# Layer 2 of a four-layer stack: where the second half's expert rows are gathered, and in which order the outputs are summed

## The chip, the cores and the metric

The kernel runs on one core of one Trainium2 chip. The metric is the device time of one launch in microseconds (us); the time before is the median of three runs. A core has five engines that each execute their own stream of instructions in order: PE (matmul, with its weight load shown as PEld), DVE (vector), ACT (scalar and activation), POOL (GpSimd) and SP, which here only issues transfers. They are tied together by semaphores. A transfer is issued by an engine (SP for plain ones, POOL for indirect ones, which take the row numbers from a tile) and carried out by the DMA queues.

## The reference, cut to what matters

x has 2048 tokens (four sequences of 512) of 256 features, all in float32. Each of four layers computes `x = x + attn(xn) + ffn(xn)` from the layernorm xn of x. The change is in layer 2:

```python
# attn: each token mixes its own 16 heads, with one key and one value
attn = softmax(einsum('blhd,bld->blh', q, k) / sqrt(hd))
out = (attn[..., None] * v[:, :, None, :]).reshape(b, l, -1)

# ffn: 8 experts, the best two for each token, and a shared one
scores = softmax(einsum('th,eh->te', xf, gate_w), axis=-1)
topk_w, topk_i = top_k(scores, 2)
topk_w = topk_w / sum(topk_w)
eo = einsum('eti,eih->eth', silu(xf @ wg) * (xf @ wu), wd)
y = einsum('te,eth->th', cw, eo)       # cw: topk_w at topk_i, else 0
shared = silu(xf @ sg) * (xf @ su) @ sd
x = x + out + y + shared
```

Layer 3 then does a causal attention with 16 heads of 128 and eight experts of another kind on the new xn.

## The kernel before, in words

x lies in SBUF as 16 tiles of 128 tokens by 256 features; a sequence is four tiles. `xnT` is the transposed layernorm, in SBUF too, from which most matmuls are fed. The normalised rows xn are also written to DRAM, as `xn_half`, one for each half of the tokens (1024).

**The experts of layer 2 by halves.** The `Half` object of each half routes its tokens (`dispatch`, L1248). It sorts the 2048 choices of 1024 tokens by expert into 23 slots of 128 rows (NS = 23): `ids` says which token each row of a slot takes, `expert` which weights a slot uses, `slot` where each token's two results lie, and `weight` what they are multiplied by. `experts` (L1366) works through the slots in twelve pairs (the last one is a single slot):

- `gather(j)` (L1373): POOL issues two indirect transfers (L1376), each of 128 rows of `xn_half` into the tile `xs`, of which there are three buffers. The gathers of pairs 0 and 1 are issued ahead of the loop, that of pair j + 2 at the start of step j.
- `turn(j)` (L1381): four PE transposes (L1386) and an ACT copy to `xsT` (L1391).
- `hidden(j)` (L1393): eight matmuls (L1398), the activation `gate` on ACT (L1405), the product `hs` on DVE (L1406).
- `turn_hidden(j)` (L1408): two PE transposes (L1412), an ACT copy to `hsT` (L1414).
- `down(j)` (L1416): four matmuls (L1420), a DVE copy to `os` (L1425), and SP's store to DRAM, `slots_out` (L1427).

`combine` (L1456) brings the results back: for each of the half's eight tiles and each of two choices POOL gathers 128 rows of `slots_out` into `row` (L1463, four buffers), and `add_scaled` (L147) adds row times weight to x on DVE (L153). When a sequence has all its sums, `part_done` starts its layernorm for layer 3 (L94: statistics on DVE at L102 and L103, the root on ACT at L90, xn on DVE at L110; later PE transposes at L121 and ACT copies to xnT).

`head_mix` (L1149) is the attention of layer 2 for one sequence: four times four matmuls (L142) with the bias added into `qkv` on DVE (L1161), a product (L1166) and a sum on DVE, a softmax, then the product `prod` on POOL (L1178), which DVE adds to x (L1183).

**The order of the work.** `weave` (L215) interleaves generators: each yields the cost of what it has just emitted, the one that has used the smallest share of its total goes next, and a start value above 0 makes a stream begin later. Layer 2 (`run`, L1500) weaves the shared expert with the two dispatches; then the first half's experts with the head mix; then the second half's experts with the first half's combine. Layer 3 (L1551) weaves the second half's combine (`rest`, L1526) with its attention and its experts. From the program so written a scheduler decides the order of each engine's instructions by its own estimates; `keep_in_program_order` ties an instruction to its place as written. On the chip every engine then follows its order strictly: an instruction that waits holds up all behind it.

At the start of layer 3 `full_attention` (L1037) computes V by projections (L142), the keys and queries of a head (L134; the bias of the queries is added on DVE, L1057), the scores (L628) and, on DVE and ACT, the softmax (L631, L635).

Of the kernel before, what the change touches and what calls it, by code (L numbers as in the profile page):

```python
# [12 lines left out]
ALU = mybir.AluOpType  # L13
AX = mybir.AxisListType

P = 128
NB, SEQ, DM = 4, 512, 256
# [65 lines left out]
def v3(ap, b):  # L83
    return ap.rearrange("p (a b) -> p a b", b=b)
# [62 lines left out]
def add_scaled(c, t, part, w=None):  # L147

    x = c.x[:, t, :]
    if w is None:  # L150
        c.nc.vector.tensor_add(x, part, x)  # L151
    else:
        c.nc.vector.scalar_tensor_tensor(x, part, w, x, ALU.mult, ALU.add)  # L153


def silu_times(c, pool, out, gate, other):
# [58 lines left out]
def weave(c, *streams, flush=True):  # L215

    live = [[start * total, total, gen] for gen, total, start in streams]
    while live:  # L220
        s = min(live, key=lambda s: s[0] / s[1])
        cost = next(s[2], None)
        if cost is None:
            live.remove(s)
        else:
            s[0] += cost
        c.step()
    if flush:
        c.step(True)
# [998 lines left out]


E8, HT, NS = 8, NTILE // 2, 23  # L1230
EW = 6 * P


class Half:
# [3 lines left out]

    def __init__(self, c, k, pool, keep, dram, hf, xn):
        self.c, self.k, self.pool, self.hf, self.xn = c, k, pool, hf, xn  # L1240
        self.out = c.tile(dram, [NS * P, DM], "slots_out")
        new = lambda shape, tag, dtype=F32: c.tile(keep, shape, tag, dtype, bufs=2)
        self.ids = new([P, NS], "ids", U32)
        self.slot = new([P, 2 * HT], "slot", U32)
        self.weight = new([P, 2, HT], "weight")
        self.expert = new([P, NS], "expert", I32)

    def dispatch(self):  # L1248
# [75 lines left out]
        for i in range(2 * HT + 4):  # L1324
# [25 lines left out]
        nc.vector.tensor_scalar(  # L1350
            where[:1], where[:1], float(E8 - 1), float(EW), ALU.min, ALU.mult
        )
# [10 lines left out]
        nc.vector.tensor_mul(w, w, tot[:, None, :].to_broadcast([P, 2, HT]))  # L1363
        yield 1.0

    def experts(self, weights, xpool, pool, opool):  # L1366


        c, nc = self.c, self.c.nc
        pairs = [[t for t in (2 * j, 2 * j + 1) if t < NS] for j in range((NS + 1) // 2)]  # L1370
        xs, xsT, hs, hT = {}, {}, {}, {}

        def gather(j):  # L1373
            xs[j] = c.tile(xpool, [P, 2, DM], "xs", bufs=3)
            for i, t in enumerate(pairs[j]):
                nc.gpsimd.indirect_dma_start(  # L1376
                    out=xs[j][:, i, :], out_offset=None, in_=self.xn,
                    in_offset=bass.IndirectOffsetOnAxis(ap=self.ids[:, t : t + 1], axis=0),
                )

        def turn(j):  # L1381
            pt = c.ps("tr")
            n = len(pairs[j])
            for i in range(n):
                for d in range(2):
                    nc.tensor.transpose(  # L1386
                        pt[:, (2 * i + d) * P : (2 * i + d + 1) * P],
                        xs[j][:, i, d * P : (d + 1) * P], c.ident,
                    )
            xsT[j] = c.tile(pool, [P, 4, P], "xsT", bufs=2)  # L1390
            nc.scalar.copy(xsT[j][:, : 2 * n, :], v3(pt[:, : 2 * n * P], P))  # L1391

        def hidden(j):  # L1393
            ph = v3(c.ps(), 2 * P)
            n = len(pairs[j])
            for i, t in enumerate(pairs[j]):
                for d in range(2):
                    nc.tensor.matmul(  # L1398
                        ph[:, i, :], lhsT=xsT[j][:, 2 * i + d, :],
                        rhs=weights[:, bass.ds(where[t] + 2 * d * P, 2 * P)],  # L1400
                        start=(d == 0), stop=(d == 1),
                    )
            sg = c.tile(pool, [P, 2, P], "gate", bufs=2)
            hs[j] = c.tile(pool, [P, 2, P], "hs", bufs=2)
            nc.scalar.activation(sg[:, :n, :], ph[:, :n, :P], AF.Silu)  # L1405
            nc.vector.tensor_mul(hs[j][:, :n, :], sg[:, :n, :], ph[:, :n, P:])  # L1406

        def turn_hidden(j):  # L1408
            pt = c.ps("tr")
            n = len(pairs[j])  # L1410
            for i in range(n):
                nc.tensor.transpose(pt[:, i * P : (i + 1) * P], hs[j][:, i, :], c.ident)  # L1412
            hT[j] = c.tile(pool, [P, 2, P], "hsT", bufs=2)
            nc.scalar.copy(hT[j][:, :n, :], v3(pt[:, : n * P], P))  # L1414

        def down(j):  # L1416
            po = v3(c.ps("acc"), DM)
            n = len(pairs[j])
            for i, t in enumerate(pairs[j]):
                nc.tensor.matmul(  # L1420
                    po[:, i, :], lhsT=hT[j][:, i, :],
                    rhs=weights[:, bass.ds(where[t] + 4 * P, DM)], start=True, stop=True,
                )
            os = c.tile(opool, [P, 2, DM], "os", bufs=2)
            nc.vector.tensor_copy(os[:, :n, :], po[:, :n, :])  # L1425
            rows = self.out[2 * j * P : (2 * j + n) * P, :]
            nc.sync.dma_start(rows.rearrange("(i p) d -> p i d", p=P), os[:, :n, :])  # L1427

        where = []
        N = len(pairs)  # L1430
        gather(0)
        gather(1)
        for lo in (0, 12):
            where.extend(nc.values_load_multi_w_load_instructions(
                self.expert[:1, lo : min(lo + 12, NS)], engines=[mybir.EngineType.PE],
                min_val=0, max_val=(E8 - 1) * EW,
                skip_runtime_bounds_check_because="the chip has limited them to the last expert's",
            )[1])
        turn(0)
        yield 0.5  # L1440
        for j in range(N + 2):
            if j + 2 < N:
                gather(j + 2)
            if j < N:
                hidden(j)
                yield 1.7
            if j + 1 < N:
                turn(j + 1)
            if j >= 2:
                down(j - 2)  # L1450
                yield 0.9
            if 1 <= j <= N:
                turn_hidden(j - 1)
            yield 0.6

    def combine(self, pool):  # L1456

        c, nc = self.c, self.c.nc
        for t in range(HT):
            tt = self.hf * HT + t  # L1460
            for r in range(2):
                row = c.tile(pool, [P, DM], "row", bufs=4)
                nc.gpsimd.indirect_dma_start(  # L1463
                    out=row, out_offset=None, in_=self.out,
                    in_offset=bass.IndirectOffsetOnAxis(
                        ap=self.slot[:, r * HT + t : r * HT + t + 1], axis=0
                    ),
                )
                add_scaled(c, tt, row, self.weight[:, r, t : t + 1])
            if tt % TPB == TPB - 1:  # L1470
                c.part_done(tt // TPB)
            yield 1.0


class Layer2:
# [23 lines left out]

    def run(self):  # L1500
        c, a = self.c, self.a
        xs, self.rows = self.pool("t_xs"), self.pool("t_rows")
        with ExitStack() as stack:
            temp, mixer = self.pool("t_temp", stack), self.pool("h_t", stack)
            unit = c.unit(a["t_shared"])
            h_small = c.tile(mixer, [P, 864], "h_small")
            c.nc.sync.dma_start(h_small, a["h_unit"])

            def dispatch():
                for half in self.halves:  # L1510
                    yield from half.dispatch()

            def mix():
                for b in range(NB):
                    yield from head_mix(c, mixer, h_small, b)

            shared = glu_pieces(c, mixer, [unit], n=2, width=256, loaded=True, bufs=4)
            experts = [half.experts(self.weights, xs, temp, self.rows) for half in self.halves]
            weave(c, (shared, 41.0, 0.0), (dispatch(), 34.0, 0.0), flush=False)
            weave(c, (experts[0], 40.0, 0.0), (mix(), 12.0, 0.0), flush=False)  # L1520
            weave(
                c, (experts[1], 40.0, 0.0), (self.halves[0].combine(self.rows), 10.0, 0.0),
                flush=False,
            )

    def rest(self):  # L1526
        yield from self.halves[1].combine(self.rows)
        self.stack.close()
# [22 lines left out]
def layer3(c, a, ahead, store):  # L1551


    def attention():
        yield from full_attention(c, a)

    def rest():
        yield from ahead
        c.parts(2, store)

    weave(
        c, (rest(), 110.0, 0.0), (attention(), 765.0, 0.0), (top_p_experts(c, a), 765.0, 0.95)
    )


# [192 lines left out]
```

## Time and profile before

| | |
|---|---|
| median of three runs | 3229.73 us |
| the three runs | 3223.44, 3234.39, 3229.73 us |
| the profiled execution | 3223.57 us, of which the span 3221.7 us |
| mean granted clock of PE | 0.988 |
| first half's experts and head mix | about 1624.5 to 1683.6 us from the span's start |
| second half's experts and first half's combine | about 1683.6 to 1749.3 us |
| indirect gathers of expert rows, L1376 | 46 on POOL, 946 ns each at the median, 3.5 us from issue to landing |
| indirect gathers of result rows, L1463 | 32 on POOL, 2.7 us from issue to landing |

The span is one execution on the chip, seen by the hardware profiler. Layer 2's experts are a small part of it, some 125 us; layers 0 and 1 lie before, layer 3 behind them. A timeline row gives the start, the duration, the engine, the line and operation, what is written from what, and in brackets how long the engine had been idle before it and what ended that. In the waits view a row names who waited, for what, how many us in total, how often, and the longest.

### The profile page before, as it was taken

Reading aid. Unit: us, or ns where it says so; the run is one execution under the profiler, and the core shown is the slowest. Engines: PE = TensorE matmul, PEld = TensorE weight load, DVE = VectorE, ACT = ScalarE, POOL = GpSimd, SP = SyncE. Lnnn points to the kernel's source line nnn. Section 1 sums busy time; section 2 is a strip of 40 time slices with the busy share of each in tenths; the row PEclk is TensorE's granted clock in tenths of the full one; section 3 lists DMA queues with packets and bytes.
Section 4 is the critical chain, followed back from the end, with each engine's and each line's share of the span. In section 5 each row is a group of like instructions: output and inputs, shape, how many; then the busy total and the mean of one; then the engine's idle time right before and its main releaser. Section 6 shows DMA issues by size and latency. Waiting matters only on the chain.

```text
span 3221.7 us, 35846 instructions
## 1 busy us (share of the span) xinstructions
PE 3099.8 (96%) x12502; PEld 1887.7 (59%) x12502; DVE 1857.9 (58%) x4730; ACT 1262.2 (39%) x2911; POOL 655.5 (20%) x525
## 2 busy tenths in 40 slices
PE   8999999998899999999997999999999999999999
PEld 4565656565555555555575565665665665555555
DVE  4777878887676777777654655545545522222222
ACT  4444444443456566657433433333333411111111
POOL 0465556556200132322044000000000000000000
PEclk9999999999999999999998999999999999999999
DMA  3232323322201244434133000000000000000000
GB/s 128 76 112 95 124 86 105 111 86 93 91 23 31 54 136 95 111 78 138 54 102 118 8 1 27 1 27 1 16 5 1 20 20 20 20 20 20 0 0 27
DMA packets 88947, 183.59 MB, mean 57 GB/s; under 512 B 14176, under 2 KB 57200, under 8 KB 84160
## 3 DMA queue, kind: packets, MB, share of 16 engines
q1 hardware_dynamic: 74304, 133.48, 12.8%
q0 software_dynamic: 14176, 47.01, 5.9%
q8 instruction: 99, 1.62, 0.2%
q10 hardware_dynamic: 288, 0.82, 0.1%
q14 instruction: 80, 0.66, 0.1%
HBM read 159.38 MB, written 12.98 MB: 53 GB/s over the span
## 4 chain that ended last, share of the span: by engine, by line
PE 73%; DVE 12%; DMA 6%; POOL 4%; ACT 3%; issue 2%; SPq 1%; DVEq 0%; ACTq 0%; POOLq 0%
PE mm L134 28%; PE acc L204 9%; PE mm L628 8%; PE mm L142 5%; PE acc L1092 4%; PE acc L644 3%; DMA G<-own 3%; DVE cy L269 2%; DVE G L410 2%; PE tr L1084 2%; PE tr L807 2%; PE acc L851 2%; PE acc L864 2%; DMA psw<-pes 1%; POOL y L459 1%
## 5 line engine op out<-in xcount | busy, mean ns | idle before, releaser
L134 PE MATMUL mm<-xnT,wu 128*128 128x512 f32 x2128 | 956.4, 596 | 7.9 <-DVE cy L269 3.4
L134 PEld LDWEIGHTS mm<-xnT,wu 128*128 128x128 f32 x2128 | 400.1, 191 | 462.7 <-issue 433.8
L635 ACT ACTIVATE pr<-pr,nm 128x128 f32<-128x128 f32 (+3 forms) x512 | 286.0, 559 | 313.3 <-DVE nm L631 310.9
L196 ACT ACTIVATE sg<-mm 128x512 f32<-128x512 f32 x168 | 99.9, 595 | 600.3 <-PE mm L134 600.1
L197 DVE TENSOR_TENSOR hT<-sg,mm 128x512 f32<-128x512 f32 x168 | 115.0, 684 | 376.1 <-PE mm L134 364.9
L204 PE MATMUL acc<-wu,hT 128*128 128x256 f32 x1344 | 304.8, 380 | 0.6 <-DVE hT L197 0.5
L631 DVE CUSTOM_DVE_ANT_0 pr<-mm,late 128x128 f32<-128x128 f32 (+3 forms) x512 | 244.6, 482 | 88.9 <-PE mm L628 84.3
L204 PEld LDWEIGHTS acc<-wu,hT 128*128 128x128 f32 x1344 | 252.2, 190 | 53.6 <-issue 20.4
L134 PE MATMUL mm<-xnT,w_in 128*128 128x512 f32 x512 | 231.5, 596 | 6.7 <-DVE cy L269 5.1
L968 POOL DMA_INDIRECT e<-in_p_experts,ids x128 | 128.1, 1001 | 494.9 <-DVE x L153 463.6
L410 DVE TENSOR_TENSOR_SCAN G<-G,eye 128x1024 f32<-128x1024 f32 x64 | 157.9, 2468 | 53.5 <-DMA G<-own 53.5
L628 PE MATMUL mm<-k,q 128*128 128x128 f32 (+3 forms) x512 | 181.0, 444 | 5.1 <-DVE q L1057 5.1
L628 PE MATMUL mm<-kf,qf 128*128 128x128 f32 (+3 forms) x512 | 176.9, 445 | 8.9 <-DVE qf L786 6.4
L436 POOL TENSOR_TENSOR G<-G,CB 128x1024 f32<-128x1024 f32 x64 | 151.1, 2361 | 141.0 <-ACT CB L362 77.6
L269 DVE SCALAR_TENSOR_TENSOR cy<-mm,ws,cy 128x509 f32<-128x509 f32 (+2 forms) x216 | 158.3, 741 | 26.2 <-ACT cy L265 22.7
L422 ACT ACTIVATE xD<-xc,ws 128x128 f32<-128x128 f32 x256 | 84.3, 391 | 198.6 <-POOL y L459 192.7
L134 PEld LDWEIGHTS mm<-xnT,w_in 128*128 128x128 f32 x512 | 96.4, 191 | 111.2 <-issue 96.5
L153 DVE SCALAR_TENSOR_TENSOR x<-acc,cw,x 128x256 f32<-128x256 f32 x128 | 61.9, 484 | 155.6 <-PE acc L204 155.6
L151 DVE TENSOR_TENSOR x<-acc,x 128x256 f32<-128x256 f32 x176 | 73.9, 421 | 134.2 <-PE acc L644 103.5
L1092 PE MATMUL acc<-PT,V 128*128 128x512 f32 (+3 forms) x512 | 149.5, 433 | 0.0
L1057 DVE TENSOR_SCALAR q<-mm,bias 128x512 f32<-128x512 f32 x64 | 48.0, 750 | 163.0 <-PE mm L134 163.0
L807 PEld LDWEIGHTS tr<-con,pr 128*128 128x128 f32 x640 | 80.9, 143 | 90.3 <-ACT pr L800 32.1
(306 smaller groups left out, 5032.3 us busy)
## 6 DMA issues: line engine op xcount, KB each, us to landing
G<-own SPq DMA_DIRECT2D x64, 512.0 KB, 4.2
w_in<-in_m_units SPq DMA_DIRECT2D x16, 1024.0 KB, 5.0
eb<-since SPq DMA_DIRECT2D x96, 128.0 KB, 3.3
wu<-in_o_units SPq DMA_DIRECT2D x8, 1536.0 KB, 6.7
wo<-in_m_units SPq DMA_DIRECT2D x16, 512.0 KB, 3.9
psw<-pes SPq DMA_DIRECT2D x128, 64.0 KB, 2.6
wu<-in_f_units SPq DMA_DIRECT2D x4, 1536.0 KB, 6.6
wu<-in_l_units SPq DMA_DIRECT2D x4, 1408.0 KB, 8.4
```

The costliest lines, as they stand in the source:

```text
L134: c.nc.tensor.matmul(out, lhsT=w[:, d, cols], rhs=c.xnT[:, d, tokens], start=(d == 0), stop=(d == 1))
L142: c.nc.tensor.matmul(out, lhsT=c.xnT[:, d, tokens], rhs=w[:, d, cols], start=(d == 0), stop=(d == 1))
L204: nc.tensor.matmul(po, lhsT=hT[k][:, t * P : (t + 1) * P], rhs=wd[:, k, :], start=(i == 0), stop=(i == per - 1),)
L269: nc.vector.scalar_tensor_tensor(y[:, j:], src[:, : SEQ - j], conv[:, k, 3 - j : 4 - j], y[:, j:], ALU.mult, ALU.add,)
L410: nc.vector.tensor_tensor_scan(flat, flat, eye.rearrange("p h t -> p (h t)"), 0.0, ALU.mult, ALU.add)
L436: nc.gpsimd.tensor_mul(G, G, seqs[b][2][:, t, :][:, None, :].to_broadcast([P, HG, P]))
L628: nc.tensor.matmul(sc, lhsT=q[:, i * P : n], rhs=k[:, :n], start=True, stop=True)
L631: nc.vector.tensor_tensor_reduce(out=pr, in0=sc, in1=late[:, SEQ - n :], scale=1.0, scalar=-NEG, op0=ALU.add, op1=ALU.min, accum_out=nm,)
L635: nc.scalar.activation(pr, pr, AF.Exp, bias=nm, scale=-1.0, accum_out=total)
L807: nc.tensor.transpose(pt[:, (i - j) * P : (i - j + 1) * P], prs[s][i][:, j * P : (j + 1) * P], c.ident)
L968: nc.gpsimd.indirect_dma_start(out=e, out_offset=None, in_=a["p_experts"], in_offset=bass.IndirectOffsetOnAxis(ap=ids[:, t, k : k + 1], ax ...
L1092: nc.tensor.matmul(z[:, j * P :], lhsT=head["V"][:, j, h, :], rhs=head["PT"][:, j, j * P :], start=(j == 0), stop=(j == TPB - 1),)
```

## The change

The first half's rows are still gathered inside its own experts, two pairs ahead, with three buffers (tag `xs0`). The second half's rows have twelve buffers of their own (tag `xs1`, one for each pair), and the generator that gathers them is a third stream beside the first half's experts and the head mix, with a total of 12 and start 0. Nothing is gathered inside the second half's experts any more. The pool of these buffers is now closed together with those of the experts and the mixer, at the end of `run`. In `combine` there are six row buffers instead of four, and the adds to x are tied to the order as written. The weights of the streams change a little: the first half's combine has a total of 11 instead of 10 and starts at 0.2 of it; the second half's combine, in layer 3, starts at 0.012 of its total.

```diff
-        c.nc.vector.tensor_add(x, part, x)
-    else:
-        c.nc.vector.scalar_tensor_tensor(x, part, w, x, ALU.mult, ALU.add)
+        return c.nc.vector.tensor_add(x, part, x)
+    return c.nc.vector.scalar_tensor_tensor(x, part, w, x, ALU.mult, ALU.add)
...
 E8, HT, NS = 8, NTILE // 2, 23
+PAIRS = [[t for t in (2 * j, 2 * j + 1) if t < NS] for j in range((NS + 1) // 2)]
...
+        self.xs = {}
...
-    def experts(self, weights, xpool, pool, opool):
-        def gather(j):
-            xs[j] = c.tile(xpool, [P, 2, DM], "xs", bufs=3)
-            for i, t in enumerate(pairs[j]):
-                nc.gpsimd.indirect_dma_start(
-                    out=xs[j][:, i, :], out_offset=None, in_=self.xn,
+    def gather(self, pool, bufs, js):
+        for j in js:
+            x = self.xs[j] = self.c.tile(pool, [P, 2, DM], f"xs{self.hf}", bufs=bufs)
+            for i, t in enumerate(PAIRS[j]):
+                self.c.nc.gpsimd.indirect_dma_start(
+                    out=x[:, i, :], out_offset=None, in_=self.xn,
                     in_offset=bass.IndirectOffsetOnAxis(ap=self.ids[:, t : t + 1], axis=0),
                 )
+            yield 1.0
+
+    def experts(self, weights, pool, opool, more):
...
-        gather(0)
-        gather(1)
+        if more:
+            next(more)
+            next(more)
...
-            if j + 2 < N:
-                gather(j + 2)
+            if more:
+                next(more, None)
...
-                row = c.tile(pool, [P, DM], "row", bufs=4)
+                row = c.tile(pool, [P, DM], "row", bufs=6)
...
-                add_scaled(c, tt, row, self.weight[:, r, t : t + 1])
+                c.tc.keep_in_program_order(
+                    add_scaled(c, tt, row, self.weight[:, r, t : t + 1])
+                )
...
-        xs, self.rows = self.pool("t_xs"), self.pool("t_rows")
+        self.rows = self.pool("t_rows")
         with ExitStack() as stack:
-            temp, mixer = self.pool("t_temp", stack), self.pool("h_t", stack)
+            xs, temp, mixer = (self.pool(name, stack) for name in ("t_xs", "t_temp", "h_t"))
...
-            experts = [half.experts(self.weights, xs, temp, self.rows) for half in self.halves]
+            first, last = self.halves
+            every = range(len(PAIRS))
+            experts = [
+                half.experts(self.weights, temp, self.rows, more)
+                for half, more in ((first, first.gather(xs, 3, every)), (last, None))
+            ]
             weave(c, (shared, 41.0, 0.0), (dispatch(), 34.0, 0.0), flush=False)
-            weave(c, (experts[0], 40.0, 0.0), (mix(), 12.0, 0.0), flush=False)
             weave(
-                c, (experts[1], 40.0, 0.0), (self.halves[0].combine(self.rows), 10.0, 0.0),
-                flush=False,
+                c, (experts[0], 40.0, 0.0), (mix(), 12.0, 0.0),
+                (last.gather(xs, len(PAIRS), every), 12.0, 0.0), flush=False,
             )
+            weave(c, (experts[1], 40.0, 0.0), (first.combine(self.rows), 11.0, 0.2), flush=False)
...
-        c, (rest(), 110.0, 0.0), (attention(), 765.0, 0.0), (top_p_experts(c, a), 765.0, 0.95)
+        c, (rest(), 110.0, 0.012), (attention(), 765.0, 0.0), (top_p_experts(c, a), 765.0, 0.95)
```

More of the change, by code (lines that the diff above doesn't have):

```diff
@@ L1364, in dispatch @@
         yield 1.0
-    def experts(self, weights, xpool, pool, opool):
-        c, nc = self.c, self.c.nc
-        pairs = [[t for t in (2 * j, 2 * j + 1) if t < NS] for j in range((NS + 1) // 2)]
-        xs, xsT, hs, hT = {}, {}, {}, {}
-        def gather(j):
-            xs[j] = c.tile(xpool, [P, 2, DM], "xs", bufs=3)
-            for i, t in enumerate(pairs[j]):
-                nc.gpsimd.indirect_dma_start(
-                    out=xs[j][:, i, :], out_offset=None, in_=self.xn,
+    def gather(self, pool, bufs, js):
[4 more added lines that the diff above has]
+                    out=x[:, i, :], out_offset=None, in_=self.xn,
                     in_offset=bass.IndirectOffsetOnAxis(ap=self.ids[:, t : t + 1], axis=0),
                 )
+            yield 1.0
+    def experts(self, weights, pool, opool, more):
+        c, nc = self.c, self.c.nc
+        pairs, xs = PAIRS, self.xs
+        xsT, hs, hT = {}, {}, {}
         def turn(j):
```

## The prediction

> **What bounds the kernel now.** I read the page's first part, then the table of windows around layer 2's experts, the waits of the bad stretch, and last the timelines of POOL, DVE and PE.
>
> ```profile
> PE 3099.8 (96%) x12502; PEld 1887.7 (59%) x12502; DVE 1857.9 (58%) x4730; ACT 1262.2 (39%) x2911; POOL 655.5 (20%) x525
> ...
> 1624.50:1644.50 20.00, 19.40 (x90) 15.11 (x89) 8.79 (x18) 5.82 (x12) 5.67 (x6) 1.00 0.36 119
> 1644.50:1683.60 39.10, 38.69 (x194) 32.09 (x193) 26.36 (x49) 17.59 (x34) 23.75 (x18) 1.00 0.44 112
> 1683.60:1749.30 65.70, 48.85 (x229) 38.54 (x228) 29.24 (x73) 25.32 (x49) 34.30 (x34) 0.90 0.40 117
> 1749.30:1763.60 14.30, 9.41 (x22) 3.80 (x20) 4.33 (x11) 4.31 (x6) 6.44 (x7) 0.98 0.50 153
> ...
> 1772.40:2400.00 627.60, 627.43 (x2358) 381.07 (x2357) 330.39 (x1152) 236.76 (x574) 15.34 (x20) 1.00 0.03 11
> ```
>
> PE is busy 96% of the span. The windows (start:end, length, busy time of PE, PEld, DVE, ACT, POOL, clock, DMA share, GB/s) show where it is not. In the first half's experts (1624.5 to 1683.6) it lacks 1 us of 59; in the second half's (1683.6 to 1749.3) it is idle for 16.9 of 65.7 us, at a granted clock of 0.90; at the start of layer 3 it is idle for 4.9. From 1772 on it is 100% busy, so whatever is won or lost up to there moves the end by the same amount. What it waits for, between 1683 and 1765 (us, times, longest):
>
> ```profile
> DVE x L153 <- DMA row<-slots_out,slot: 26.3, 17, 8.0
> ...
> ACT rsq L90 <- DVE mv L103: 6.4, 1, 6.4
> ...
> PE mm L1398 <- ACT xsT L1391: 5.5, 4, 4.4
> ...
> PE mm L628 <- DVE q L1057: 4.9, 1, 4.9
> ```
>
> DVE stands 26.3 us at the adds of combine for gathered rows; hs, os and the layernorm stand behind them, ACT stands behind mv (6.4), and PE behind ACT (4.4 in one piece). POOL, which feeds all, shows (start, duration):
>
> ```profile
> 1634.56 0.94 POOL L1376 DMA_INDIRECT xs<-xn_half,ids  x1 [18.33 <-PE tr L1386]
> ...
> 1647.02 1.93 POOL L1178 TENSOR_TENSOR prod<-s,qkv 128x1024 f32<-128x1024 f32 x1
> ...
> 1655.42 1.86 POOL L1376 DMA_INDIRECT xs<-xn_half,ids  x1 [2.96 <-PE tr L1386]
> ...
> 1697.73 1.01 POOL L1376 DMA_INDIRECT xs<-xn_half,ids  x1 [0.30 <-issue]
> 1699.05 0.95 POOL L1376 DMA_INDIRECT xs<-xn_half,ids  x1 [0.30 <-issue]
> 1700.30 0.95 POOL L1463 DMA_INDIRECT row<-slots_out,slot  x1 [0.30 <-DVE st L102]
> ```
>
> A gather holds POOL 0.95 us plus 0.30, a pitch of 1.25 us. From 1691.7 to 1733 POOL does nothing else, expert rows and combine rows mixed: it is the narrow place of the second half.
>
> **What the skill says.** (1) "SBUF — State Buffer", section "SBUF: two separate sides": POOL writes the descriptors of a gather, and is locked out while DVE holds the shared port pair. The trace agrees: the gather at 1655.42 took 1.86 us beside the 1.23 us product L1166 on DVE, against 0.95. (2) "DMA: Bandwidth & Descriptors", "Anatomy of one DMA — SWDGE (gpsimd) path": about 2.0 us fixed plus bytes over 436 GB/s, so 2.3 us for 128 KB. The trace has 2.7 (rows) and 3.5 us (xs) at the median from issue to landing; I use these. (3) "TensorE: Matmul & The Clock Gate", "What's actually happening": the array is at half rate after an idle window of about 3.4 us and needs as much busy time to come back. The trace agrees: after 4.39 us idle, eight matmuls of L1398 took 3.78 us against 1.89.
>
> **The change, part by part.** In the order in which the changed program issues on POOL, the first half's pairs 0 to 3 come first, then all 23 gathers of the second half in one block, and only then the first half's pairs 4 to 7, prod of sequence 0, pairs 8 to 10, prod 1, pair 11, prods 2 and 3, then the combine rows. PE's and SP's orders in the first half are unchanged.
>
> *Loss in the first half.* The block needs the second half's ids: DVE writes them at 1621.8 to 1622.0, so POOL starts near 1622.8 (0.8 for semaphore and issue). 23 x 1.25 = 28.75, plus 0.9 for the one gather that meets the product L1166 (1.86 - 0.95): pair 4's two gathers start at 1652.4 and 1653.7 instead of 1634.6 and 1635.8. With 3.5 us to landing the second tile is there at 1657.2, where PE turned it at 1644.15: PE stands some 13 us. Behind pairs 4 to 7 (8 x 1.25, to 1662.2) comes prod 0 with 1.93, to 1664.1; in the trace of before it ended at 1648.95. DVE's x L1183 (1.22) waits for it with qkv (0.36 until the next) and pair 4's hs (0.4) behind it, so pair 4's turn_hidden, at 1651.63 before, comes near 1666.2: **+14.6**. PE was 38.7 of 39.1 us busy up to 1683.6, so nothing takes this back. The array is cold after the idle time; part of it falls into the wait for prod 0: +1.0, between 0 and 1.7 (half of 3.4 us).
>
> *Gain in the second half.* All its tiles have landed by then, and POOL only has rows to fetch. The start up to turn_hidden of pair 2 stays, without the 1.65 us wait: 1696.6 on before's clock. The seven pairs to pair 9 then go at PE's own pace, 1.73 (hidden) + 0.44 (turn) + 0.87 (down) + 0.22 (turn_hidden) = 3.26 us, as the first half showed: 22.8. One set of L121 transposes adds 0.9; from pair 9's turn_hidden (1743.80) to the stretch's end at 1749.3 before had 5.5, less the 0.9 of sequence 1's transposes, which now come later: 4.6. Sum 1724.9; with 0.7 for small waits 1725.6, so 65.7 becomes 42.0: **-23.7**. What must hold: rows come at 1.25 us each, two adds to a pair, 2.5 of 3.26 us; DVE has 2 x 0.48 for them, 0.68 (os), 0.41 (hs) and about 1.0 for bn and xn, 3.1 of 3.26. The first row can be issued at 1691.7 + 14.6 = 1706.3 and lands by 1710, where pair 3's hs, the first PE work behind it, is due near 1714. Pinning the adds costs nothing as long as the rows keep this pace; the two further row buffers let POOL run ahead by 2.5 us.
>
> *Start of layer 3.* DVE's q L1057 now stands before the four row adds that it waited behind. Its 4.94 us of PE idle become about 1: -3.9. L628 (4.61 for 8) and L134 (4.49, warm 3.60) ran cold; L628's four matmuls took 0.89 later, so at most 2.8 + 0.9 is to be had; I take 2.0, as the clock's windows run free. The moved L121 adds 0.9. Sum **-5.0**, between -6.7 and -2. The later start of the second half's combine (0.012) moves nothing on PE except this; wo's load behind the last down is as before.
>
> Edits with one answer: add_scaled's return value, the global PAIRS and the pools' nesting issue no instruction: nothing.
>
> **Sum.** 14.6 + 1.0 - 23.7 - 5.0 = **-13.1 us**. The profiled execution took 3223.6 (span 3221.7), so it would be 3210.5; the median of before, 3229.7, lies 6.2 above it and goes to **3216.5**.
>
> **Rivals.**
> B. The block costs less: were the second half's gathers hidden, or pair 4 not stopped, the gains stand alone, -28 to -29: 3201. For it: the 20 us of idle POOL before 1634. Against: pair 4 stands behind the block in POOL's order, and PE has nothing ahead of turn(4).
> C. The other side: the second half stays as long, since DVE still runs in order and each late row, pinned now, holds hs and os. Each pair would wait for rows at the trace's 8 to 9 us per pair; then 14.6 + 1.0 - 5.0 = +10.6: 3240. It decides once the stretch shrinks by less than 10.6 us. For it: the 26.3 us of row waits. Against: most of them were rows held up behind expert gathers on POOL, which are gone.
> D. The gathers of the block run slower than 1.25: at the trace's longest, 1.97 + 0.30, for all of them 23 us would be added; for 16 us (a pitch of 1.95) the sum is +3: 3233. Break-even is a pitch of 1.82. For it: DVE's port. Against: only one wide SBUF product falls into the block.
> That the change does not do what it says is excluded by POOL's order.
>
> **How the numbers follow.** Chances: forecast 0.60, B 0.10, C 0.17, D 0.13. About 0.3% (9.7 us) is what a measurement of this kernel can tell from no change. The forecast's own spread is 3207 to 3226 (block 12 to 17, second half -17 to -26, layer 3 -2 to -6.7), so a quarter of it falls within 0.3%: 0.45 faster, 0.15 same. B adds 0.10 to faster; C, at the line itself, 0.05 to same and 0.12 to slower; D 0.03 faster, 0.06 same and 0.04 slower. Faster 0.58, same 0.26, slower 0.16. The range 3203 to 3236 leaves out most of B and of C.
>
> **What would show it.** POOL: 23 gathers in a row from about 1623 to 1652, then pair 4's. PE: one idle stretch of 12 to 14 us before turn(4), and a second short one before pair 4's turn_hidden. The second half's experts: PE near 40 of 42 us, clock near 1.0, DVE's row waits no longer passed on to PE. q before the row adds. It is wrong if turn(4) is not late (B), if PE in the second half still stands over 10 us (C), or if the block's pitch is over 1.5 (D).

## The result, and the profile after

| | before | after |
|---|---|---|
| median, us | 3228.45 (3219.24 to 3234.39, 6 runs) | 3210.61 (3201.8 to 3218.45, 6 runs) |
| ratio, 95% interval | | 0.995 (0.9927 to 0.9973) |
| profiled execution's span, us | 3221.7 | 3210.0 |

The changed kernel is faster by 0.5%, about 18 us, with an interval of 9 to 24 us; the forecast was 13.

Single executions of this kernel differ by some 15 us, so the comparison of two profiles needs marks inside the program. Three are easy to find in every PE timeline: the first turn_hidden of the first half (two transposes of hs), the first transpose of the second half's rows, and the first matmul of V in layer 3 (mm from wu and xnT, L142). With the first transpose of pr in layer 3 as the end they make three stages, which I call first half, second half and start of layer 3. The windows view cut at these marks, before:

```profile
1637.76:1683.61 45.85, 45.44 (x231) 37.96 (x230) 31.09 (x58) 20.98 (x40) 26.83 (x22) 1.00 0.42 108
1683.61:1746.95 63.34, 46.49 (x221) 36.83 (x220) 28.24 (x72) 24.78 (x47) 34.30 (x34) 0.89 0.40 117
1746.95:1772.37 25.42, 20.48 (x48) 9.93 (x47) 11.45 (x36) 8.15 (x17) 11.47 (x13) 0.87 0.42 129
```

and after:

```profile
1646.16:1706.02 59.86, 47.88 (x230) 39.39 (x229) 31.01 (x58) 21.11 (x40) 33.33 (x29) 0.89 0.40 101
1706.02:1746.37 40.35, 38.70 (x213) 32.87 (x211) 27.40 (x66) 21.29 (x42) 18.66 (x17) 1.00 0.42 125
1746.37:1765.64 19.27, 18.34 (x57) 9.26 (x56) 8.75 (x31) 10.81 (x21) 7.66 (x8) 1.00 0.49 145
```

(start:end, length, then busy time of PE, PEld, DVE, ACT and POOL, PE's granted clock, DMA share, GB/s.) The first half has grown by 14.0 us, the second has shrunk by 23.0 and the start of layer 3 by 6.2: together 15.1 us less. PE's idle time and its low clock have moved from the second half to the first: 17 us of idle and a clock of 0.89 there before, 12 us and 0.89 here after.

The rest of the spans' difference lies where the change has moved nothing. The first expert gather comes at 1592.94 us before and at 1601.29 after (8.35 later), and from the first transpose of pr to the end there are 1449.3 us before and 1444.4 after (5.0 less; before had a window of 300 us at a clock of 0.98 in it). 8.35 - 15.1 - 5.0 = -11.7, the difference of the spans. Both ends of this sum are taken for the chance of one execution. For the first, the profiles of the kernels below bear this out: over all 13 the first gather comes between 1586.2 and 1608.9 us. The second is less sure. The piece from the first transpose of pr to the end takes 1444.4 to 1444.7 us in eight of them and 1449.3 to 1451.4 in five; those five have, about 740 us into it, 20 us at a clock of 0.72 to 0.80, with PE busy throughout. The three kernels that move no gathers are all among the five, and two of the ten others, so it stays open whether the change has a part in these 5 us. The medians fit either way: 15.1 and 20.1 us both lie between 9 and 24.

POOL in the changed kernel, in the timeline (start, duration, operation, idle time before):

```profile
1630.62 0.95 POOL L1372 DMA_INDIRECT xs<-xn_half,ids  x1 [6.04 <-DVE tot L1363]
...
1648.16 1.93 POOL L1372 DMA_INDIRECT xs<-xn_half,ids  x1 [0.30 <-issue]
...
1660.41 0.94 POOL L1372 DMA_INDIRECT xs<-xn_half,ids  x1 [0.30 <-issue]
1661.66 0.95 POOL L1372 DMA_INDIRECT xs<-xn_half,ids  x1 [0.30 <-issue]
...
1670.13 1.95 POOL L1177 TENSOR_TENSOR prod<-s,qkv 128x1024 f32<-128x1024 f32 x1
```

The block runs from 1630.62 to 1660.1; only the gather at 1648.16 takes longer. It meets a product on DVE:

```profile
1648.05 1.22 DVE L1165 TENSOR_TENSOR prod<-qkv 128x1024 f32<-128x1024 f32 x1
```

Pair 4's two gathers are those at 1660.41 and 1661.66. PE's timeline shows what waits for them:

```profile
1650.60 1.89 PE L1402 MATMUL mm<-weights,xsT 128*128 x8
1664.07 1.22 PE L1390 MATMUL tr<-con,xs 128*128 128x128 f32 x4 [11.58 <-DMA xs<-xn_half,ids]
1665.08 1.91 PE L1424 MATMUL acc<-weights,hsT 128*128 x4
1666.79 2.13 PE L142 MATMUL mm<-h_small,xnT 128*128 128x288 f32 x4
...
1674.04 0.38 PE L1416 MATMUL tr<-con,hs 128*128 128x128 f32 x2
```

PE stands 11.58 us before turn(4), and runs the next three groups at half speed (1.22, 1.91 and 2.13 us, where the same groups took 0.60, 1.03 and 1.13 before).

In the second half and at the start of layer 3 four waits stood out before: DVE's of 26.3 us for rows, ACT's of 6.4 for mv, PE's of 5.5 for xsT and of 4.9 for q. After, from 1706 to 1768, ACT's root of a layernorm no longer waits for mv at all, and of the others this is left (who, for what, us in total, times, longest):

```profile
PE mm L1402 <- ACT xsT L1395: 1.5, 3, 1.0
...
PE mm L627 <- DVE q L1056: 1.1, 2, 0.9
...
DVE x L152 <- DMA row<-slots_out,slot: 0.8, 1, 0.8
```

### The profile page after: what moved, and what is told of

It reads as the page before. It is cut to its first block, busy times and chain, and to the rows that moved or that the text cites. A ratio compares the mean times of both kernels' runs of the same rounds, so it can differ in the third digit from the quotient of the medians.

```text
span 3210.0 us, 35838 instructions
## 1 busy us (share of the span) xinstructions
PE 3093.7 (96%) x12502; PEld 1888.0 (59%) x12502; DVE 1858.1 (58%) x4730; ACT 1262.3 (39%) x2910; POOL 653.1 (20%) x525
## 4 chain that ended last, share of the span: by engine, by line
PE 74%; DVE 12%; DMA 5%; POOL 4%; ACT 3%; issue 2%; SPq 1%; DVEq 0%; ACTq 0%; POOLq 0%
PE mm L134 28%; PE acc L203 8%; PE mm L627 8%; PE mm L142 5%; PE acc L1091 4%; PE acc L643 3%; DMA G<-own 3%; DVE cy L268 2%; DVE G L409 2%; PE tr L1083 2%; PE tr L806 2%; PE acc L850 2%; PE acc L863 2%; POOL y L458 1%; DMA psw<-pes 1%
## 5 line engine op out<-in xcount | busy, mean ns | idle before, releaser
L134 PE MATMUL mm<-xnT,wu 128*128 128x512 f32 x2128 | 958.5, 597 | 7.4 <-ACT sg L388 2.9
L134 PEld LDWEIGHTS mm<-xnT,wu 128*128 128x128 f32 x2128 | 400.4, 191 | 461.2 <-issue 432.6
L134 PE MATMUL mm<-xnT,w_in 128*128 128x512 f32 x512 | 232.7, 598 | 7.2 <-DVE cy L268 5.1
L134 PEld LDWEIGHTS mm<-xnT,w_in 128*128 128x128 f32 x512 | 97.2, 192 | 112.4 <-issue 97.8
L495 PE MATMUL tr<-wo,y 128*128 128x256 f32 x512 | 128.8, 395 | 9.1 <-DVE x L151 3.5
```

The costliest lines, as they stand in the source:

```text
L134: c.nc.tensor.matmul(out, lhsT=w[:, d, cols], rhs=c.xnT[:, d, tokens], start=(d == 0), stop=(d == 1))
L495: nc.tensor.matmul(po, lhsT=y[:, k, :], rhs=groups[i][1][:, k, :], start=(k == 0), stop=(k == 3))
```

## The experiments

The lengths of the three stages in us, each from the PE timeline of that kernel's profile, with the ratio of the times to the kernel before and its interval:

| kernel | first half | second half | start of layer 3 | sum against before | ratio |
|---|---|---|---|---|---|
| before | 45.85 | 63.34 | 25.42 | | 1 |
| after | 59.86 | 40.35 | 19.27 | -15.1 | 0.995 (0.9927 to 0.9973) |
| own12 | 52.25 | 40.34 | 19.27 | -22.8 | 0.9917 (0.9901 to 0.9933) |
| sums_only | 45.84 | 48.83 | 19.27 | -20.7 | 0.9936 (0.9924 to 0.9948) |
| gathers_only | 60.38 | 55.79 | 24.16 | +5.7 | 1.0 (0.9992 to 1.0008) |
| rest_at_0 | 58.43 | 40.34 | 24.35 | -11.5 | 0.9959 (0.9944 to 0.9974) |
| block12 | 45.85 | 43.22 | 19.26 | -26.3 | 0.9919 (0.9899 to 0.994) |
| block16 | 50.75 | 44.48 | 19.27 | -20.1 | 0.9939 (0.9915 to 0.9962) |
| own12_block16 | 45.85 | 42.89 | 19.27 | -26.6 | 0.9929 (0.9911 to 0.9947) |
| own12_block20 | 45.85 | 40.63 | 19.27 | -28.9 | 0.9917 (0.9897 to 0.9937) |
| unpinned | 60.44 | 53.50 | 28.75 | +8.1 | 1.002 (1.001 to 1.0029) |
| row4 | 60.16 | 40.35 | 19.26 | -14.8 | 0.9937 (0.9915 to 0.996) |
| tie_only | 45.85 | 54.84 | 25.16 | -8.8 | 0.9963 (0.9948 to 0.9978) |

In all but before, sums_only and tie_only, POOL issues gathers of the second half as a block among those of the first.

### Which half of the change brings the gain: sums_only and gathers_only

The change is two things: where the second half's rows are gathered, and how the sums of combine are placed. Each was built alone. sums_only is the kernel before with

```diff
-                row = c.tile(pool, [P, DM], "row", bufs=4)
+                row = c.tile(pool, [P, DM], "row", bufs=6)
...
-                add_scaled(c, tt, row, self.weight[:, r, t : t + 1])
+                c.tc.keep_in_program_order(
+                    add_scaled(c, tt, row, self.weight[:, r, t : t + 1])
+                )
...
-                c, (experts[1], 40.0, 0.0), (self.halves[0].combine(self.rows), 10.0, 0.0),
+                c, (experts[1], 40.0, 0.0), (self.halves[0].combine(self.rows), 11.0, 0.2),
...
-        c, (rest(), 110.0, 0.0), (attention(), 765.0, 0.0), (top_p_experts(c, a), 765.0, 0.95)
+        c, (rest(), 110.0, 0.012), (attention(), 765.0, 0.0), (top_p_experts(c, a), 765.0, 0.95)
```

and add_scaled returning its instruction; gathers_only is the changed kernel with these lines as before.

> The kernel before with the changed combine alone (adds tied to the order as written, six row buffers, combine's later starts); the second half's rows are gathered in its own experts as before. DVE's order is that of the changed kernel, POOL's nearly that of before. Theory (POOL's pace of 1.25 us a gather is what holds the second half): 27 of the 31 gathers must still be issued before the last pair's rows, so the second half's stretch is 52 to 54 us (65.7 before, about 42 changed); nothing is lost in the first half; with 6 us at the start of layer 3 about 18 us faster than before, 0.994. Rival 1 (the order of the adds on DVE was all that held it): 42 us, 0.991. Rival 2 (only the gathers count): 65 us, 0.998.

> The changed gathers alone; combine as before (four row buffers, adds free to be placed, no later starts). POOL's order is that of the changed kernel, DVE's nearly that of before, with three to four row adds ahead of each hs. Theory: the first half loses 14 us; the second half's adds come 1.25 us apart and hold hs by 4 to 5 us a pair for the first four pairs, so its stretch is about 47 us; the start of layer 3 gains nothing: 4 us faster than before, 0.999. Rival (POOL cleared is enough): stretch 42 us, 0.997. Other rival (the order of the adds is what counts): stretch 60 us or more, 1.003.

sums_only took 0.9936 of before, where 0.994 was expected, and its second half 48.83 us, shorter than the 52 to 54 of the theory, but held by the same thing: POOL never stops there, and PE waits for expert rows. From its timelines of POOL and PE:

```profile
1710.09 0.94 POOL L1462 DMA_INDIRECT row<-slots_out,slot  x1 [0.30 <-issue]
...
1712.59 0.95 POOL L1462 DMA_INDIRECT row<-slots_out,slot  x1 [0.30 <-DMA xs<-xn_half,ids]
1713.84 0.95 POOL L1375 DMA_INDIRECT xs<-xn_half,ids  x1 [0.30 <-issue]
```

```profile
1710.53 0.41 PE L1385 MATMUL tr<-con,xs 128*128 128x128 f32 x2 [1.71 <-DMA xs<-xn_half,ids]
1712.30 0.69 PE L1385 MATMUL tr<-con,xs 128*128 128x128 f32 x2 [1.36 <-DMA xs<-xn_half,ids]
```

gathers_only has the reverse fault: POOL only has rows to fetch, but DVE's order still puts two to six adds ahead of an hs. Its second half took 55.79 us (47 expected), and PE's timeline names who was late:

```profile
1717.39 0.41 PE L1416 MATMUL tr<-con,hs 128*128 128x128 f32 x2 [2.02 <-DVE hs L1410]
1720.96 3.41 PE L1402 MATMUL mm<-weights,xsT 128*128 x8 [3.15 <-ACT xsT L1395]
...
1735.22 1.11 PE L1390 MATMUL tr<-con,xs 128*128 128x128 f32 x4 [4.83 <-ACT xnT L126]
```

The last two waits, 8.0 us together, were not in any expectation of this run. They come by way of ACT, as the forecast had read it in the kernel before. In ACT's order the root of a layernorm, and the loading of its table, stand ahead of the copies xsT and xnT, and both wait for mv, the statistics of a sequence whose rows DVE has added late. ACT's timeline of gathers_only:

```profile
1720.14 0.30 ACT L90 ACTIVATE rsq<-mv,eps 128x4 f32<-128x4 f32 x1 [4.35 <-DVE mv L103]
...
1731.41 1.28 ACT L90 ACT_TABLE_LOAD   x1 [4.52 <-DVE mv L103]
```

ACT waits there 6.38 and 4.49 us in the kernel before, 4.62 and 4.82 in unpinned, and not at all in the changed kernel.

Of the second half's 23.0 us, the order of the sums alone brings 14.5 and the gathers alone 7.6; both theories that named one cause alone fall. And the gathers alone cost 14.5 us in the first half: by itself that part of the change gains nothing, 1.0 with an interval of 0.9992 to 1.0008. With this block it gains nothing on top of the sums either: it takes 8.5 us off the second half and adds 14.0 to the first, so the stages of the changed kernel are 5.6 us longer than those of sums_only (the times, 0.995 and 0.9936, don't separate the two). The stages of gathers_only's one profile say +5.7 us; the timed runs show 0 within 2.6. From the first transpose of pr to the end this profile is 4.8 us shorter than that of before, which would close most of the gap if it came of the change; that is open.

### Why the first half loses: own12, block12, block16

The theory: pair 4's gather stands behind the block because the first half's rows have three buffers, and the loss is what the block reaches past the moment at which POOL is needed. own12 gives the first half twelve buffers:

```diff
-                for half, more in ((first, first.gather(xs, 3, every)), (last, None))
+                for half, more in ((first, first.gather(xs, len(PAIRS), every)), (last, None))
```

> The changed kernel with twelve buffers for the first half's rows as well, so that all its 23 gathers stand before the second half's block. Theory (pair 4's rows are late because, with three buffers, its gather stands behind the block): PE's idle stretch before turn(4), 11.6 us in the changed kernel, is gone. The block then holds prod of sequence 0 instead, to about 5 us later than before, so 5 of the 14 us of loss stay: about 9 us faster than the changed kernel, 0.992 of before. Rival (the block's transfers themselves slow down whatever runs beside them): the loss stays near 14 us, 0.995 of before.

The idle time before turn(4) is gone, and 6.4 us of the loss stay where they were expected, at prod of sequence 0, which now stands behind the block. POOL's, DVE's and PE's timelines of own12:

```profile
1659.30 0.95 POOL L1372 DMA_INDIRECT xs<-xn_half,ids  x1 [0.30 <-issue]
1660.27 1.93 POOL L1177 TENSOR_TENSOR prod<-s,qkv 128x1024 f32<-128x1024 f32 x1
```

```profile
1662.24 1.22 DVE L1182 TENSOR_TENSOR x<-x,prod 128x1024 f32<-128x1024 f32 x1 [7.19 <-POOL prod L1177]
1663.38 0.45 DVE L1160 TENSOR_TENSOR qkv<-mm,h_small 128x288 f32<-128x288 f32 x1
```

```profile
1663.98 3.75 PE L1402 MATMUL mm<-weights,xsT 128*128 x8 [3.40 <-DVE qkv L1160]
```

The line is to be read from the top: the last gather of the block, prod behind it, DVE 7.19 us idle until prod is there, then qkv, and PE waiting 3.40 us for qkv and running cold after it (3.75 us for eight matmuls of L1402, else 1.89).

The length of the block was then varied with the number of buffers of the second half's rows, the first half keeping its three:

```diff
-                (last.gather(xs, len(PAIRS), every), 12.0, 0.0), flush=False,
+                (last.gather(xs, 6, every), 12.0, 0.0), flush=False,
```

(8 in block16).

> The changed kernel with six instead of twelve buffers for the second half's rows, so that the block ahead of the first half's pair 4 holds 12 gathers instead of 23; the other 11 follow as turns free buffers. Theory (a threshold: the loss is what the block, at 1.25 us a gather, reaches past the time at which pair 4 and prod need POOL): the block ends near pair 4's time of before, the first half loses 0 to 2 us; only 7 of the 11 late gathers fall behind prod of sequence 3, so the second half stays at 40 to 42 us: about 27 us faster than before, 0.9915. Rival (the loss is in proportion to the gathers moved): 7 us lost, 0.9935. Second rival (any gather left in the second half costs as in the kernel before): stretch 48 us, 0.994.

> The changed kernel with eight buffers for the second half's rows: a block of 16 gathers, 20 us. Theory (threshold): pair 4's second tile comes 3.4 us late and prod of sequence 0, behind pairs 4 to 7, 5 to 6 us late: the first half loses 5 to 6 us, second half 40 to 42 us; about 22 us faster than before, 0.993. Rival (in proportion to the gathers): 10 us lost.

With 12, 16 and 23 gathers in the block the first half loses 0.0, 4.9 and 14.0 us. It is a threshold: the first 12 cost nothing, and from 16 to 23 each costs 9.1 / 7 = 1.30 us, near the pitch of 1.25 (the five kernels with the same block of 23 and three buffers lose 12.6 to 14.6 us, so 1.1 to 1.4). In proportion to the gathers, 12 would have cost 7.3 us. The second half grows a little, to 43.22 and 44.48 us, where 40 to 42 were expected: a pair of expert gathers stands between combine's first and second row, the second add comes late, and hs stands behind it. PE of block12:

```profile
1706.88 0.41 PE L1416 MATMUL tr<-con,hs 128*128 128x128 f32 x2 [2.34 <-DVE hs L1410]
```

### What a version without the loss is worth: own12_block16, own12_block20

Both have own12's line, and eight or ten buffers for the second half's rows.

> Twelve buffers for the first half's rows and eight for the second's: the first half's 23 gathers first, then 16 of the second's, which end before prod of sequence 0 needs POOL. Theory: the first half loses nothing (own12 lost 6 us there, at prod), the second half takes 40 to 42 us, the start of layer 3 gains 6 to 7: about 29 us faster than before, 0.991, the best of all. Rival (own12's 6 us in the first half do not come from prod behind the block): 0.992 to 0.993.

> Twelve buffers for the first half's rows, ten for the second's: 23 gathers, then a block of 20, whose end falls 1 to 2 us after the time at which prod of sequence 0 needs POOL; the last three gathers stand before prod of sequence 3, none among combine's rows. Theory: 0 to 2 us lost in the first half, and the second half at 40.4 us again instead of 42.9 (with block16, one gather pair stands between combine's first and second row, and hs waits 2.3 us there): the experts and the start of layer 3 together 26 to 28 us shorter than before, 0.9915. Rival (the 42.9 us come from the smaller number of buffers as such): 42 to 43 us.

With a block of 16 the first half loses nothing, so own12's 6.4 us did come from prod behind the block. The second half is at 42.89 us, with the same wait of hs as in block12, so the time expected for it, 29 us below before, was not reached: 26.6 us by the stages, and 0.9929, which lies in the rival's range. It is the length of the first half that decides against the rival. With a block of 20 no expert gather stands among the rows; the second half is back at 40.63 us, and the rival, that fewer buffers cost as such, falls. The first half loses nothing there either. The windows of own12_block20:

```profile
1654.92:1700.77 45.85, 45.44 (x231) 37.95 (x229) 31.03 (x58) 20.99 (x40) 13.85 (x11) 1.00 0.25 79
1700.77:1741.40 40.63, 38.88 (x212) 32.80 (x211) 27.19 (x66) 21.27 (x42) 20.25 (x20) 1.00 0.49 134
1741.40:1760.67 19.27, 18.33 (x56) 9.26 (x55) 8.72 (x31) 10.81 (x21) 7.88 (x8) 1.00 0.45 146
```

PE is busy 102.7 of these 105.75 us at full clock: little is left. Its stages are 28.9 us shorter than those of before and 13.7 shorter than those of the changed kernel. The times alone (0.9917, 0.9897 to 0.9937) put it clearly below the kernel before; from the changed kernel (0.9927 to 0.9973) and from own12 and block12 they don't separate it, the intervals overlap. The same holds for sums_only, which moves no gathers: by the stages own12_block20 is 8.2 us shorter, so the gathers are worth that much once their block costs nothing, but the times (0.9924 to 0.9948 for sums_only) don't show it.

### What makes the order of the sums: rest_at_0, unpinned, tie_only, row4

rest_at_0 is the changed kernel with the second half's combine at 0.0 in layer 3; unpinned is the changed kernel without the tie of the adds; tie_only is the kernel before with that tie and nothing else; row4 is the changed kernel with four row buffers.

> The changed kernel with the second half's combine starting at 0 in layer 3, as before. Theory (q stands behind four row adds, which wait for rows): 5 to 7 us of PE idle and cold clock come back at the start of layer 3, 0.997 of before, first half and second half as in the changed kernel. Rival (the start of layer 3 gained because the stretch before it ended in better order): no change against the changed kernel, 0.995.

> The changed kernel without tying the adds of combine to the order as written; six row buffers and the later starts stay. In DVE's order two to four row adds again stand ahead of each hs, and eight ahead of the first queries of layer 3. Theory (the tie is what brings the gain of the order): second half near 55 us as with the gathers alone, the start of layer 3 slower than before: 1.000 to 1.004 of before. Rival (the row buffers and the later starts bring it): 0.995 as in the changed kernel.

> The kernel before with the adds of combine tied to the order as written, and nothing else: four row buffers, combine's streams starting at 0. The adds are then spread evenly, but the first four to eight still stand ahead of hs of the second and third pair, and four ahead of layer 3's queries. Theory (the tie and the later start of combine make the order together): second half between 50 and 58 us (48.8 with both, 63.3 before), the start of layer 3 as before: 8 to 12 us faster than before, 0.997. Rival (the tie alone does it): 49 us, 0.9955.

> The changed kernel with four row buffers instead of six. Theory (two rows are needed in 3.26 us, and a row is issued, landed and added within 5 us, so four are enough): second half within 1 us of the changed kernel's 40.4; 0.995 of before, as the changed kernel. Rival (the buffers let POOL run ahead, and that is part of the gain): second half 43 us or more.

rest_at_0 loses 5.1 us at the start of layer 3 (24.35 against 19.27) and nothing in the second half. DVE and PE there:

```profile
1753.53 0.48 DVE L152 SCALAR_TENSOR_TENSOR x<-row,weight,x 128x256 f32<-128x256 f32 x1 [6.66 <-DMA row<-slots_out,slot]
...
1758.54 0.72 DVE L1056 TENSOR_SCALAR q<-mm,bias 128x512 f32<-128x512 f32 x1
```

```profile
1759.41 4.08 PE L627 MATMUL mm<-k,q 128*128 128x128 f32 x8 [4.33 <-DVE q L1056]
```

PE ends the last matmul (L134) before this gap at 1755.1, but the adds stand ahead of q in DVE's order, the first row lands only at 1753.5 and the fourth add starts at 1757.5. unpinned loses 22.6 us of the 29.1 that the changed kernel gains in these two stages: its second half takes 53.50 us, and at the start of layer 3 seven adds stand ahead of q in the trace (eight were expected, four stood there before), which costs more than in the kernel before (28.75 against 25.42):

```profile
1774.56 2.26 PE L627 MATMUL mm<-k,q 128*128 128x128 f32 x5 [7.47 <-DVE q L1056]
```

(The line counts only the first five of these matmuls; all eight took 4.61 us.) tie_only shows that the tie is not all of it: 54.84 us, since combine, starting at 0, still puts its first adds ahead of hs of the second and third pair (PE waits 1.65 and 1.48 us there), and mv of the first sequence comes late enough for ACT's root to wait 3.84 us for it and PE 4.88 us behind ACT. The tie, combine's later start and six row buffers make the 48.8 of sums_only. row4 shows that in the changed kernel the two further buffers are not needed: 40.35 us, to the hundredth as with six.

## Why the prediction was right, point by point

*The order of POOL and the block.* Right. On before's clock (8.35 us earlier than in the profile after) pair 4's first gather came at 1652.06; the forecast said 1652.4. prod ended at 1663.7, against 1664.1.

*The loss in the first half*: 14.6 and 1.0 for the cold array, in sum 15.6; measured 14.0. The sum holds, but its two terms are made up differently. turn(4) was 11.8 us late (20.14 less 8.35), not 13. Then the cold array cost 2.3 us, from turn(4) to pair 4's turn_hidden (9.97 us, before 7.70), more than the 0 to 1.7 that the forecast allowed: PE worked for nearly 5 us at half speed, up to the matmuls at 1669.07, where the forecast had 3.4. prod's chain, which the forecast let decide, was ready at the same moment: hs of pair 4 was written from 1673.63 on, and PE took it at 1674.04 without the second idle stretch that the forecast had named as a sign. So the cold array was not on top of the wait for prod but beside it, and the term of +1.0 that was set on top was the one too many. That the two paths end together is chance. own12 shows the same chain of prod alone.

*The gain in the second half*: -23.7 forecast, -23.0 measured, with five pairs in a row at PE's own pace of 3.25 us. The number was right, the reason given for it only in part. In rival C it was held against the rival that most row waits "were rows held up behind expert gathers on POOL, which are gone". gathers_only takes the expert gathers away and leaves DVE's order, and 15.4 of the 23.0 us stay; sums_only does the reverse, and 8.5 stay. The order in which DVE does the adds was the larger part. The forecast had counted on both, as one step, so the sum was not touched. "Pinning the adds costs nothing" understated it: without the tie the kernel is slower than before (1.002, 1.001 to 1.0029).

*The start of layer 3*: -5.0 forecast, -6.2 measured; PE waits 0.94 us for q instead of 4.94, and nothing runs cold any more, where the forecast had taken only 2.0 of up to 3.7 us for that. rest_at_0 gives 5.1 of the 6.2 us back, so this gain is in the main that of combine's later start.

*The two further row buffers* and the other small edits were put at nothing, which row4 bears out for the buffers.

*The rivals.* B (no block cost) needs a change that the kernel doesn't have: block12 and own12_block20 show it, at 26 and 29 us by the stages, where B had worked out 28 to 29. C did not happen: DVE's new order spreads the adds to two a pair, and without that order (unpinned) the kernel is slower than before. D did not: of the 23 gathers one took 1.93 us and all others about 0.95.

*The times.* The stages give -15.1 us, the medians -17.8 with an interval of 9 to 24; the forecast of -13.1 lies within. The three stages were each forecast to within 1.6 us, so the sum owes little to errors that cancel.

*Small slips in the working.* 3229.7 less 13.1 is 3216.6, not 3216.5. The parts given for the forecast's own spread lead to 3209 to 3228, not to 3207 to 3226. The pairs that C takes at 8 to 9 us took 8.7 to 9.9. And POOL's unbroken row of gathers before ends at 1727.6, not at 1733: it is idle for 5.39 us ahead of the last one. None of these would have changed the direction of the forecast.

On what the Trainium skill says in "TensorE: Matmul & The Clock Gate", "What's actually happening", of half rate after an idle window, this case agrees on the rate: 11.58 us of idle, then three groups in 5.26 us that took 2.76 before. The lengths that the prediction takes from there, about 3.4 us each, fit less well: nearly 5 us of work were at half speed here, and in the kernel before eight matmuls of L1398 took 3.16 us (from 1705.84; else 1.89) after three pieces of idle time of only 0.77, 1.05 and 1.30 us.

## What to carry to other kernels

Work moved ahead into a queue's idle time is free only up to the moment at which that queue is next needed: count what is behind it in the same order, in gathers times pitch, and stop there; here 12 cost nothing, 23 cost 14 us, and the buffers of the moved work set the length. An in-order engine that adds up results as they arrive passes each late arrival on to all that stands behind it; spreading such adds to the pace at which rows land, behind the work that PE waits for, was worth more than making the rows land sooner. And where a change moves two orders at once, build each alone: here one half gained 21 us by itself, and the other nothing.

## What was not expected of the hardware

The pitch of a gather on POOL stayed at 1.25 us even through 43 to 46 of them almost in a row (own12 and own12_block20), with only the one that meets a wide product of DVE much longer, 1.56 to 1.96 us. In all 13 profiles together 56 gathers begin while a product of 128 x 1024 is running on DVE, and 54 of them end 0.81 to 0.87 us behind it, whether they began 0.04 or 1.1 us into it: in own12 the product ends at 1649.42 and the gather, begun at 1648.68, at 1650.24. (The two others, in rest_at_0, took 0.94 us, beside a product that took 1.29 us instead of 1.22.) The reduction of as many elements that DVE does next held no gather: in own12 it runs from 1649.46 to 1650.68, and this gather ends in the midst of it. And parts of the program that the change does not touch differed by 5 to 8 us between two profiled executions, about half of what was to be measured; without marks inside the program the two spans alone (11.7 us apart) would have misjudged the stages, which gained 15.1.
